# Routed experts of an SSM and mixture-of-experts kernel: gate and up weights become the stationary operand

## The chip, the cores and the metric

The kernel runs on one core of a Trainium2 chip. The metric is the device time of one launch in microseconds: the median of 3 runs. Lower is better. The profile is one further execution, taken by the hardware profiler; a profile has a span, which is the time from the core's first to its last instruction.

## What is computed

The input x has 128 sequences of 32 channels (heads) of 512 positions, all 32-bit floats. First, a state-space layer makes a kernel of 512 taps for each channel from its parameters, convolves each row causally with it, adds D times the input and sets everything from the sequence's length on to zero. The lengths lie between 78 and 453. Then the 4096 rows (sequence and channel) of 512 values are the tokens of a mixture of experts: 16 routed experts, 4 of them for each token, and a shared one for all.

```python
scores = sigmoid(x @ gate_w.T) + bias
topk_w, topk_idx = top_k(scores, 4)
topk_w = topk_w / (sum(topk_w) + 1e-20)
z   = silu(x @ Wg[e].T) * (x @ Wu[e].T)        # for every expert e of the token; 512 -> 256
out = sum over e of (z * weight of e) @ Wd[e].T   # 256 -> 512
out = out + silu(x @ Sg.T) * (x @ Su.T) @ Sd.T    # the shared expert
result = input + out
```

## The kernel before

The work has three stages. In the first (to about 122 us) TensorE convolves (L611), turns the results, and VectorE (DVE) works out the routing. The convolved rows go to a tensor in DRAM, `y_rows`, with the token's 16 expert weights behind each row's 512 values. They also stay on the chip, turned, as `yT`. The sequences are ranked by length, longest first.

In the second stage (to about 264 us, `unit_step`, L1114) the shared expert runs over `yT` in eight units of 512 tokens. Beside it the list of routed work is made (`slots`): tokens sorted by expert, in tiles of 128, each tile filled from one expert only. There are 128 to 143 tiles, depending on the routing.

The third stage (`turn_of`, L1267) runs over the tiles in a software pipeline that is written out by hand. Instructions are issued in the order of the program text on every engine (`tc.manual_schedule(engines=None)`, L1258), so what stands ahead of an instruction on its engine is read from the text. One step does this:

- POOL gathers the token rows of the tile four steps ahead from `y_rows` (L1037), with an indirect DMA.
- `tokens(step)`: TensorE transposes the 128 rows in blocks of 128 positions (L1168), ScalarE (ACT) copies the result to `yt` (L1174), and DVE picks each token's weight for the tile's expert, `wt` (L1175).
- `order(step - 2)`: SyncE (SP) marks when the rows that a tile adds to are free (L1251 to L1256).
- `turn(step - 2)`: two transposes of the tile's z (L1218), copied by DVE to `zT` (L1221).
- `inner(step - 1)`: the gate and up products. `yt` is the stationary operand, the weights move, 512 columns at once (gate and up side by side): one product for each position block (L1200). ACT takes the silu (L1211), DVE multiplies silu, up and token weight to z (L1212).
- `outer(step - 2)`: two down products (L1226), DVE's copy to `ob` (L1235), and POOL's indirect DMA that adds the rows to the output (L1236).
- `registers(step + 1)`: TensorE loads two numbers into registers: where the tile's expert lies in the ring of weights (`woff`, L1191), and how many blocks of 128 positions the longest sequence of the tile reaches, `k` from 1 to 4 (`ntk`, L1194).
- SP loads one more expert into the ring, if this tile is the first of its expert (L1286 to L1289).

The positions are stored in reverse, so that the used blocks are the last k of 4. `by_tiles` (L1044) makes the branches on k: two nested conditions with a full body for each value of k. A branch only exists for TensorE here; the other engines do the same work for every k. What a body signals to other engines has to be the same for each way through it, because those wait for a fixed count of TensorE's completions.

The weights of an expert (`WSZ`, 3072 columns on 128 partitions: gate and up in four blocks of 512, then down) lie in a ring of `R` = 8 places in the tile `store`. In the second stage `yT` and the shared expert's weights lie in the same tile. A place is loaded (L1145, L1146) once the units that it covers are through (`free_after`, L1107).

The 128 tiles that always exist are followed by those that the routing may need: there (`rest`, L1301) every engine first loads a register that says whether there is one more tile.

Of the kernel before, what the change touches and what calls it, by code (L numbers as in the profile page):

```python
# [28 lines left out]
F32 = mybir.dt.float32  # L29
# [3 lines left out]
AF = mybir.ActivationFunctionType  # L33
ALU = mybir.AluOpType
# [4 lines left out]
P = 128  # L39
B, H, L, N = 128, 32, 512, 64  # L40
E, TOPK, I = 16, 4, 256
KT = L // P
IT = I // P
# [4 lines left out]
NU = B // UB  # L48
TU = UB * H
NC2 = H * N // P  # L50
PAD = P
YW = L + E
R = 8
SPARE = 16
ONE_HOTS = 8
WARM = 16
# [7 lines left out]
WSZ = 2 * KT * I + IT * L  # L64
# [15 lines left out]
def ssm_moe_kernel(  # L80
# [15 lines left out]
    nc = tc.nc  # L96
# [3 lines left out]
    big = ctx.enter_context(tc.tile_pool(name="big", bufs=1))  # L100
    sp = ctx.enter_context(tc.tile_pool(name="sp", bufs=2))
    d1 = ctx.enter_context(tc.tile_pool(name="d1", bufs=1, space=bass.MemoryType.DRAM))
    ps_m = ctx.enter_context(tc.tile_pool(name="ps_m", bufs=2, space=PSUM))
    ps_g = ctx.enter_context(tc.tile_pool(name="ps_g", bufs=2, space=PSUM))
    ps_u = ctx.enter_context(tc.tile_pool(name="ps_u", bufs=2, space=PSUM))
# [16 lines left out]
    for j in range(2):  # L122
# [17 lines left out]

    store = big.tile([P, 3 * WSZ + KT * H * P], F32, tag="store", name="store")
    yT = store[:, 2 * WSZ : 2 * WSZ + KT * H * P].rearrange(
        "p (u k h b) -> p u k h b", u=NU, k=KT, h=H
    )
    w_sh = store[:, 2 * WSZ + KT * H * P :]
    ring_flat = store[:, : R * WSZ]
    y_rows = d1.tile([B * H, YW], F32, tag="y_rows", name="y_rows")
    out_bh = out[: B * H, :].rearrange("(b h) l -> b h l", h=H)  # L150
    y_bh = y_rows.rearrange("(b h) w -> b h w", h=H)
# [6 lines left out]
    def dep(of, on, why):  # L158
        tc.add_manual_dep(of.ins, on.ins.name, SYNC, reason=why)


    ident = const.tile([P, P], F32, tag="ident", name="ident")
# [584 lines left out]
    made = {}  # L747

    def slots():
# [53 lines left out]
        for n in range(1, KT):  # L803
# [12 lines left out]
        nc.vector.tensor_scalar(  # L816
            marks[:, 1, :], num[:E, :], float(R - 1), uend, ALU.add, ALU.is_ge
        )
        nc.vector.tensor_scalar(marks[:, 2, : R - 1], t_e[:, : R - 1], uend, None, ALU.is_ge)

# [13 lines left out]
        for k in range(TOPK):  # L834
# [10 lines left out]
        nc.tensor.matmul(  # L845
            pl[:, 1, : R - 1], lhsT=ones[:E, :], rhs=marks[:, 2, : R - 1], start=True, stop=True
        )
# [150 lines left out]
    with tc.manual_schedule(engines={mybir.EngineType.PE}):  # L998
        for h, n in [(0, 1), (1, 1), *((h, 2) for h in range(2, H, 2))]:
            tb, q = divmod(h, HB)  # L1000
# [18 lines left out]
    gp = ctx.enter_context(tc.tile_pool(name="gp", bufs=2))  # L1019
# [7 lines left out]
    def homes(pool, tag, shape, n):  # L1027

        return [pool.tile(shape, F32, tag=tag, name=f"{tag}_{i}", bufs=n) for i in range(n)]

    def at(tiles, t):
        return tiles[t % len(tiles)]
# [11 lines left out]
    def by_tiles(k_t, some):  # L1044


        with tc.If(k_t > 2) as many:
            with tc.If(k_t > 3) as all4:
                some(4)
            with all4.Else():  # L1050
                some(3)
        with many.Else():
            with tc.If(k_t > 1) as two:
                some(2)
            with two.Else():
                some(1)
# [49 lines left out]

    def free_after(j):  # L1107

        return min((max(j - 1, 0) * WSZ - 1) // (KT * TU), NU - 1)

    making = slots()
    gathered = 0
# [36 lines left out]
    w0s, k_ts = {}, {}  # L1149

    yt = homes(gp, "yt", [P, KT, P], 2)
    wts = homes(gp, "wt", [P, 1], 4)
    junks = homes(gp, "junk", [P, E], 2)
    sgs = homes(gp, "sgt", [P, I], 2)
    zs = homes(gp, "zt", [P, I], 2)
    zts = homes(gp, "zT", [P, IT, P], 2)
    p_t, p_gu = homes(ps_m, "m", [P, KT, P], 2), homes(ps_g, "g", [P, 2 * I], 2)
    p_z = homes(ps_u, "u", [P, IT, P], 2)

    marks = {}  # L1160

    def tokens(t):

        pt = at(p_t, t)

        def transposes(n):
            for q in range(KT - n, KT):
                nc.tensor.transpose(pt[:, q, :], at(yg, t)[:, q * P : (q + 1) * P], ident)  # L1168

        if t < len(p_t):  # L1170
            transposes(KT)
        else:
            by_tiles(k_ts[t], transposes)
        nc.scalar.copy(at(yt, t), pt)  # L1174
        nc.vector.scalar_tensor_tensor(  # L1175
            at(junks, t),
            epos,
            made["texp"][:, t : t + 1],
            at(yg, t)[:, L:],
            ALU.is_equal,  # L1180
            ALU.mult,
            accum_out=at(wts, t),
        )

    def in_ring(t, mm):
        for other in loads[t + 1 :]:
            tc.declare_no_dep(mm.ins, other.ins, reason="another place of the ring")
        dep(mm, loads[t], "the tile's expert")

    def registers(t):  # L1190
# [2 lines left out]
        )  # L1193
        k_ts[t] = nc.tensor.value_load(made["ntk"][0:1, t : t + 1], min_val=1, max_val=KT)  # L1194

    def inner(t):
        pgu = at(p_gu, t)
        def products(n):
            for q in range(KT - n, KT):
                mm = nc.tensor.matmul(  # L1200
                    pgu,
                    lhsT=at(yt, t)[:, q, :],
                    rhs=ring_flat[:, bass.ds(w0s[t] + q * 2 * I, 2 * I)],
                    start=(q == KT - n),
                    stop=(q == KT - 1),
                )
                in_ring(t, mm)

        by_tiles(k_ts[t], products)
        sg = at(sgs, t)  # L1210
        nc.scalar.activation(sg, pgu[:, :I], AF.Silu)  # L1211
        nc.vector.scalar_tensor_tensor(  # L1212
            at(zs, t), pgu[:, I:], at(wts, t), sg, ALU.mult, ALU.mult
        )

    def turn(t):
        for it in range(IT):
            nc.tensor.transpose(  # L1218
                at(p_z, t)[:, it, :], at(zs, t)[:, it * P : (it + 1) * P], ident
            )  # L1220
        nc.vector.tensor_copy(at(zts, t), at(p_z, t))  # L1221

    def outer(t):
        po = at(p_o, t)
        for it in range(IT):
            mm = nc.tensor.matmul(  # L1226
                po,
                lhsT=at(zts, t)[:, it, :],
                rhs=ring_flat[:, bass.ds(w0s[t] + WD + it * L, L)],
                start=(it == 0),  # L1230
                stop=(it == IT - 1),
            )
            in_ring(t, mm)
        ob = at(obs, t)
        nc.vector.tensor_copy(ob, po)  # L1235
        add = nc.gpsimd.indirect_dma_start(  # L1236
            out=out,
            out_offset=bass.IndirectOffsetOnAxis(ap=made["put"][:, t : t + 1], axis=0),
            in_=ob,
            in_offset=None,  # L1240
            compute_op=ALU.add,
        )
        dep(add, marks[t], "the rows it adds to")
        for other in adds:
            tc.declare_no_dep(add.ins, other.ins, reason="other rows, or behind the mark")
        adds.append(add)
# [11 lines left out]
    with tc.manual_schedule(engines=None):  # L1258

        dep(nc.tensor.nop(), parts_last[0], "in TensorE's order")  # L1260
        for u in range(NU):
            unit_step(u)
        for _ in making:
            pass
        registers(0)

        def turn_of(step):  # L1267
            if step + AHEAD < NT:
                gather(step + AHEAD)
            else:  # L1270
                nc.gpsimd.nop()
            if step < NT:
                tokens(step)
            if step >= 2:
                order(step - 2)
                turn(step - 2)
            if 1 <= step <= NT:
                inner(step - 1)
            if step >= 2:
                outer(step - 2)  # L1280
            if step + 1 < NT:
                registers(step + 1)
            if 1 <= step < NT:

                t = step - 1
                e = nc.sync.value_load(made["lexp"][0:1, t : t + 1], min_val=0, max_val=E - 1)  # L1286
                to = nc.sync.value_load(made["loff"][0:1, t : t + 1], min_val=0, max_val=(R - 1) * WSZ)
                go = nc.sync.value_load(made["load"][0:1, t : t + 1], min_val=0, max_val=1)
                ld = load_expert(e, ring_flat[:, bass.ds(to, WSZ)], go)  # L1289
                for other in loads:  # L1290
                    tc.declare_no_dep(ld.ins, other.ins, reason="another place of the ring")
                loads.append(ld)

        turn_of(0)
        unit_step(NU)
        for step in range(1, NT_MIN + 2):
            if step == LAST_DRAIN:
                nc.gpsimd.drain(fusable=False)
            turn_of(step)

        def rest(step):  # L1301

            if step == NT + 2:
                return
            _, (some,) = nc.values_load_multi_w_load_instructions(
                made["full"][0:1, step - 2 : step - 1], min_val=0, max_val=1
            )
            with tc.If(some > 0):
                turn_of(step)
                rest(step + 1)  # L1310

        rest(NT_MIN + 2)
# [51 lines left out]
```

## Time and profile before

| | |
|---|---|
| median of 3 runs | 913.76 us (913.17 to 913.97) |
| the profiled execution | 913.5 us |
| its span, mean granted TensorE clock | 911.8 us, 0.992 |
| busy share of the span: TensorE products, its weight loads, DVE, ACT, POOL | 96%, 49%, 45%, 21%, 46% |
| the routed stage | from 264 us to about 900 us |
| products L1200 and L1226, transposes L1168 and L1218: records | 742, 536, 373, 268 |

PE is TensorE and PEld its weight loads; PEldq and PEq are its sequencer, which reads the instructions. A group's line reads: source line, engine, operation, output and inputs by their names, number of records; then busy microseconds and the mean nanoseconds of one; then the idle time before them and what ended it. The ends of products are modelled, so their mean is longer than their pace. The chain of work that ended last goes back from the last instruction to what released it; a line of it reads: start, microseconds, engine, output, line, number. A 32-bit product shows as two records, each with its weight load, a transpose as one; a few records can be missing.

### The profile page before, as it was taken

To read this page: it belongs to the slowest core of one execution; us is meant where nothing else is said; L and a number is where in the kernel's file an instruction comes from. 1 tells how busy PE (TensorE), PEld (TensorE's weight loads), DVE (VectorE), ACT (ScalarE), POOL (GpSimd) and SP (SyncE) were. 2 spreads that over 40 slices of the span, in tenths; PEclk is the share of its full clock that TensorE was granted. 3 is DMA by queue.
4 is the path that set the end of the run, shared out by engine and by line. 5 is a ranking of instruction groups with operands and counts; after the bars stand their busy time and mean duration, and the time that the engine had idled before them with its cause. 6 is when DMAs were issued, how large, how long until landed. Compare 5 with 4: busy or idle time off the path is not lost.

```text
span 911.8 us, 14680 instructions
## 1 busy us (share of the span) xinstructions
PE 872.7 (96%) x2976; PEld 445.0 (49%) x2976; DVE 414.7 (45%) x1488; ACT 188.8 (21%) x379; POOL 420.1 (46%) x372
## 2 busy tenths in 40 slices
PE   2999999999999999999999999999999999999994
PEld 1677654444444444445444444444444545444441
DVE  8988664968802334333342334333333323344332
ACT  1222221111231112211221122112221112122221
POOL 2210011422473556645564456545654455566554
PEclk9999999999999999999999999999999999999997
DMA  5688576786698667766677667656756556667575
GB/s 198 216 279 274 185 242 193 207 197 124 125 218 202 141 114 131 165 135 114 120 140 171 113 110 140 114 110 108 141 108 108 107 96 117 109 129 136 105 127 98
DMA packets 54710, 136.03 MB, mean 149 GB/s; under 512 B 12432, under 2 KB 12592, under 8 KB 50992
## 3 DMA queue, kind: packets, MB, share of 16 engines
q0 software_dynamic: 36256, 89.77, 53.4%
q1 hardware_dynamic: 14096, 36.15, 11.8%
q10 hardware_dynamic: 4224, 8.39, 2.5%
q8 instruction: 76, 1.25, 0.5%
q14 instruction: 58, 0.48, 0.2%
HBM read 288.08 MB, written 60.64 MB: 382 GB/s over the span
## 4 chain that ended last, share of the span: by engine, by line
PE 92%; DVE 2%; SPq 2%; issue 2%; POOL 0%; ACT 0%; DMA 0%; ACTq 0%; DVEq 0%; POOLq 0%
PE g L1200 35%; PE o L1226 24%; PE o L1087 6%; PE py L611 6%; PE g L1072 5%; PE u L1072 4%; PE m L1168 4%; PE u L1218 3%; PE pt L635 1%; PE pa L902 1%; PE parts L656 1%; PE pg L673 1%; SPq L1251 1%; DVE wq L269 0%; PE py L446 0%
## 5 line engine op out<-in xcount | busy, mean ns | idle before, releaser
L1200 PE MATMUL g<-store,yt 128*128 x742 | 343.1, 596 | 1.9 <-issue 1.4
L1236 POOL DMA_INDIRECT out<-ob,put x134 | 212.1, 1583 | 234.5 <-DVE junk L1175 186.8
L1226 PE MATMUL o<-store,zT 128*128 x536 | 252.0, 592 | 0.0
L1212 DVE SCALAR_TENSOR_TENSOR zt<-g,wt,sgt 128x256 f32<-128x256 f32 x135 | 65.3, 484 | 305.2 <-ACT sgt L1211 301.6
L1200 PEld LDWEIGHTS g<-store,yt 128*128 128x128 f32 x742 | 130.3, 190 | 118.9 <-issue 117.8
L1226 PEld LDWEIGHTS o<-store,zT 128*128 128x128 f32 x536 | 101.4, 190 | 128.7 <-issue 124.3
L1037 POOL DMA_INDIRECT yg<-y_rows,get x140 | 138.1, 986 | 49.8 <-issue 30.8
L1235 DVE COPY ob<-o 128x512 f32<-128x512 f32 x134 | 92.6, 691 | 109.3 <-PE o L1226 99.5
L1174 ACT COPY yt<-m 128x512 f32<-128x512 f32 x136 | 79.6, 585 | 226.0 <-PE m L1168 216.2
L1211 ACT ACTIVATE sgt<-g 128x256 f32<-128x256 f32 x135 | 51.7, 383 | 268.8 <-PE g L1200 227.5
L1096 POOL DMA_INDIRECT out<-ob,unit_rows x32 | 50.2, 1567 | 92.6 <-ACT ob L1094 57.6
L1168 PEld LDWEIGHTS m<-ident,yg 128*128 128x128 f32 x373 | 48.7, 141 | 72.2 <-issue 71.7
L611 PE MATMUL py<-strip,xt 128*128 128x192 f32 (+7 forms) x256 | 63.6, 403 | 0.0
L1168 PE MATMUL m<-ident,yg 128*128 128x128 f32 x373 | 63.0, 273 | 0.5 <-issue 0.4
L1087 PE MATMUL o<-store,z 128*128 128x512 f32 x128 | 57.6, 597 | 0.6 <-issue 0.6
L1221 DVE COPY zT<-u 128x256 f32<-128x256 f32 x134 | 56.2, 419 | 0.5 <-issue 0.4
L611 PEld LDWEIGHTS py<-strip,xt 128*128 128x128 f32 x256 | 44.2, 194 | 18.5 <-issue 13.2
L1218 PE MATMUL u<-ident,zt 128*128 128x128 f32 x268 | 51.2, 273 | 0.6 <-DVE zt L1212 0.6
L1072 PE MATMUL g<-store 128*128 128x512 f32 x92 | 42.9, 601 | 1.5 <-issue 1.2
L1072 PE MATMUL u<-store 128*128 128x512 f32 x92 | 42.2, 593 | 0.0
L914 DVE TENSOR_SCALAR cols<-tpos_h,stl,tok 128x143 f16<-128x143 f16 x128 | 41.4, 328 | 0.0
L1087 PEld LDWEIGHTS o<-store,z 128*128 128x128 f32 x128 | 23.4, 190 | 26.3 <-issue 26.2
(285 smaller groups left out, 490.6 us busy)
## 6 DMA issues: line engine op xcount, KB each, us to landing
store<-in_w_all SPq DMA_DIRECT2D x143, 1536.0 KB
xt<-in_x_t SPq DMA_DIRECT2D x8, 1024.0 KB
y_rows<-yb ACTq DMA_DIRECT2D x8, 1024.0 KB
out<-in_x POOLq DMA_DIRECT2D x8, 1024.0 KB
strip<-kd SPq DMA_DIRECT2D x7, 1024.0 KB
yg<-y_rows,get POOLq DMA_INDIRECT x140
out<-ob,put POOLq DMA_INDIRECT x134
strip<-kd SPq DMA_DIRECT2D x4, 256.0 KB
```

The costliest lines, as they stand in the source:

```text
L611: nc.tensor.matmul(py[:, c0 : L - jt * P], lhsT=xt[:, jt, q, :], rhs=strip[tb][:, q, jt * P + c0 :], start=(jt == 0), stop=(jt == KT - 1 o ...
L1037: nc.gpsimd.indirect_dma_start(out=at(yg, t), out_offset=None, in_=y_rows[:, :], in_offset=bass.IndirectOffsetOnAxis(ap=made["get"][:, t : ...
L1072: nc.tensor.matmul(ps[it], lhsT=w_sh[:, c0 : c0 + P], rhs=yT[:, u, kt, :, :].rearrange("p h b -> p (h b)"), start=(kt == KT - n), stop=(kt ...
L1087: nc.tensor.matmul(po, lhsT=at(zu, u)[:, it, q * P : (q + 1) * P], rhs=w_sh[:, c0 : c0 + L], start=(it == 0), stop=(it == IT - 1),)
L1168: nc.tensor.transpose(pt[:, q, :], at(yg, t)[:, q * P : (q + 1) * P], ident)
L1174: nc.scalar.copy(at(yt, t), pt)
L1200: mm = nc.tensor.matmul(pgu, lhsT=at(yt, t)[:, q, :], rhs=ring_flat[:, bass.ds(w0s[t] + q * 2 * I, 2 * I)], start=(q == KT - n), stop=(q = ...
L1212: nc.vector.scalar_tensor_tensor(at(zs, t), pgu[:, I:], at(wts, t), sg, ALU.mult, ALU.mult)
L1218: nc.tensor.transpose(at(p_z, t)[:, it, :], at(zs, t)[:, it * P : (it + 1) * P], ident)
L1226: mm = nc.tensor.matmul(po, lhsT=at(zts, t)[:, it, :], rhs=ring_flat[:, bass.ds(w0s[t] + WD + it * L, L)], start=(it == 0), stop=(it == IT ...
L1235: nc.vector.tensor_copy(ob, po)
L1236: add = nc.gpsimd.indirect_dma_start(out=out, out_offset=bass.IndirectOffsetOnAxis(ap=made["put"][:, t : t + 1], axis=0), in_=ob, in_offse ...
```

## The change

The gate and up products swap their operands. The weights become the stationary operand, four squares of 128 by 128 for each position block, and the tokens move, 128 columns at a time. The result is z with its 256 features on the partitions, which is the form that the down products need: `turn` and its transposes go away.

[...] `fetch(step)`, at the start of a step, copies the expert's gate and up weights from the ring to one of two tiles `fixed`: ACT copies the blocks 0 and 1, DVE the blocks 2 and 3, each 1024 columns, after a register load of `woff` on its own engine. The copy for a tile is issued one step before its products.

With features on the partitions the token's weight can't be applied at z any more; DVE's product for z becomes a plain product of silu and up, and the weight is applied at the output's copy, where tokens lie on the partitions.

The branches on k are written anew: the last block always; if k > 1, block 1 if k > 2, block 0 if k > 3, and block 2 at the end; otherwise the last block alone. The two tiles take room, so the ring has 7 places instead of 8, and `yT` begins at column 2048 of the tile instead of 6144 (`Y0`), which changes when a place may first be loaded.

```diff
-R = 8
+R = 7
...
-    store = big.tile([P, 3 * WSZ + KT * H * P], F32, tag="store", name="store")
-    yT = store[:, 2 * WSZ : 2 * WSZ + KT * H * P].rearrange(
-        "p (u k h b) -> p u k h b", u=NU, k=KT, h=H
-    )
-    w_sh = store[:, 2 * WSZ + KT * H * P :]
-    ring_flat = store[:, : R * WSZ]
+    store = big.tile([P, R * WSZ], F32, tag="store", name="store")
+    Y0 = R * WSZ - WSZ - KT * H * P
+    yT = store[:, Y0 : Y0 + KT * H * P].rearrange("p (u k h b) -> p u k h b", u=NU, k=KT, h=H)
+    w_sh = store[:, Y0 + KT * H * P :]
+    ring_flat = store
+
+    fixed = [big.tile([P, KT, 2 * I], F32, tag=f"fixed{i}", name=f"fixed{i}") for i in range(2)]
...
-        return min((max(j - 1, 0) * WSZ - 1) // (KT * TU), NU - 1)
+        return min(((j + 1) * WSZ - Y0 - 1) // (KT * TU), NU - 1)
...
+    def fetch(t):
+
+        for engine, copy, q0 in (
+            (nc.scalar, nc.scalar.copy, 0),
+            (nc.vector, nc.vector.tensor_copy, KT // 2),
+        ):
+            w0 = engine.value_load(made["woff"][0:1, t : t + 1], min_val=0, max_val=(R - 1) * WSZ)
+            half = KT // 2 * 2 * I
+            op = copy(
+                at(fixed, t)[:, q0 : q0 + KT // 2, :].rearrange("p k w -> p (k w)"),
+                ring_flat[:, bass.ds(w0 + q0 * 2 * I, half)],
+            )
+            in_ring(t, op)
+
     def inner(t):
-        pgu = at(p_gu, t)
-        def products(n):
-            for q in range(KT - n, KT):
-                mm = nc.tensor.matmul(
-                    pgu,
-                    lhsT=at(yt, t)[:, q, :],
-                    rhs=ring_flat[:, bass.ds(w0s[t] + q * 2 * I, 2 * I)],
-                    start=(q == KT - n),
-                    stop=(q == KT - 1),
-                )
-                in_ring(t, mm)
-
-        by_tiles(k_ts[t], products)
+
+        pgu, w = at(p_gu, t), at(fixed, t)
+
+        def products(q, start, stop):
+
+
+            for g in range(2):
+                for it in range(IT):
+                    c0 = g * I + it * P
+                    first, end = (g, it) == (0, 0), (g, it) == (1, IT - 1)
+                    nc.tensor.matmul(
+                        pgu[:, g, it, :],
+                        lhsT=w[:, q, c0 : c0 + P],
+                        rhs=at(yt, t)[:, q, :],
+                        start=start and first,
+                        stop=stop and end,
+                    )
+
+        last, more = KT - 1, k_ts[t]
+        with tc.If(more > 1) as several:
+            products(last, True, False)
+            with tc.If(more > 2):
+                products(1, False, False)
+                with tc.If(more > 3):
+                    products(0, False, False)
+            products(2, False, True)
+        with several.Else():
+            products(last, True, True)
         sg = at(sgs, t)
-        nc.scalar.activation(sg, pgu[:, :I], AF.Silu)
-        nc.vector.scalar_tensor_tensor(
-            at(zs, t), pgu[:, I:], at(wts, t), sg, ALU.mult, ALU.mult
-        )
-
-    def turn(t):
-        for it in range(IT):
-            nc.tensor.transpose(
-                at(p_z, t)[:, it, :], at(zs, t)[:, it * P : (it + 1) * P], ident
-            )
-        nc.vector.tensor_copy(at(zts, t), at(p_z, t))
+        nc.scalar.activation(sg, pgu[:, 0], AF.Silu)
+        nc.vector.tensor_mul(at(zs, t), sg, pgu[:, 1])
...
-                lhsT=at(zts, t)[:, it, :],
+                lhsT=at(zs, t)[:, it, :],
...
-        nc.vector.tensor_copy(ob, po)
+        nc.vector.tensor_scalar(ob, po, at(wts, t), None, ALU.mult)
...
             if step < NT:
+                fetch(step)
                 tokens(step)
             if step >= 2:
                 order(step - 2)
-                turn(step - 2)
             if 1 <= step <= NT:
                 inner(step - 1)
```

## The prediction

> **What bounds the kernel now.** I read the chain that ended last, then the groups, then the order of time inside the routed stage, which runs from 264 us to about 900 us of the 911.8 us span. The chain, by engine and by line:
>
> ```profile
> PE 92%; DVE 2%; SPq 2%; issue 2%; POOL 0%; ACT 0%; DMA 0%; ACTq 0%; DVEq 0%; POOLq 0%
> PE g L1200 35%; PE o L1226 24%; PE o L1087 6%; PE py L611 6%; PE g L1072 5%; PE u L1072 4%; PE m L1168 4%; PE u L1218 3%; PE pt L635 1%; PE pa L902 1%; PE parts L656 1%; PE pg L673 1%; SPq L1251 1%; DVE wq L269 0%; PE py L446 0%
> ```
>
> TensorE is the bound, and the changed products (L1200) with the removed transposes (L1218) are 38% of the chain. The groups show what one instruction costs on each engine:
>
> ```profile
> L1200 PE MATMUL g<-store,yt 128*128 x742 | 343.1, 596 | 1.9 <-issue 1.4
> ...
> L1235 DVE COPY ob<-o 128x512 f32<-128x512 f32 x134 | 92.6, 691 | 109.3 <-PE o L1226 99.5
> L1174 ACT COPY yt<-m 128x512 f32<-128x512 f32 x136 | 79.6, 585 | 226.0 <-PE m L1168 216.2
> ...
> L1221 DVE COPY zT<-u 128x256 f32<-128x256 f32 x134 | 56.2, 419 | 0.5 <-issue 0.4
> L1218 PE MATMUL u<-ident,zt 128*128 128x128 f32 x268 | 51.2, 273 | 0.6 <-DVE zt L1212 0.6
> ```
>
> The 596 ns is a latency. The chain between 600 and 610 us shows the pace, in a step whose tile needs k=3 position blocks:
>
> ```profile
> 599.89 2.58 PE g L1200 x6
> 602.47 1.72 PE o L1226 x4
> 604.19 0.33 PE m L1168 x3
> 604.51 0.22 PE u L1218 x2
> 604.73 2.58 PE g L1200 x6
> ```
>
> Six records in 2.58 us are 0.43 us each: a 32-bit product is two records, each with its own weight load. A transpose is one record of 0.11. So a step costs 0.11k + 0.22 + 0.86k + 1.72 us: 4.84 for k=3, 5.81 for k=4, 3.88 for k=2. The chain has 28 steps with k=4, 54 with k=3 (mean 4.854), 44 with k=2 (mean 3.947) and 9 with k=1 (about 3.25). Only short steps have holes, as here around 453 us (k=2):
>
> ```profile
> 452.43 0.22 PE m L1168 x2
> 452.65 0.22 PE u L1218 x2
> 452.87 0.10 issue
> 452.97 1.95 PE g L1200 x4
> ```
>
> "Issue" is the instruction front end of TensorE (its sequencer), which works in order. Its own records:
>
> ```profile
> L1191 PEldq TENSOR_LOAD <-woff x137: 297/306/662, 261.8 to 897.1; - x137
> ...
> L1194 PEldq SEQ_ASSERT  x137: 18/18/18, 263.2 to 898.4; - x137
> ...
> L1048 PEldq COMPARE_BRANCH  x364: 65/179/358, 122.7 to 879.2; - x182
> ```
>
> The two register loads of a step take it from 261.8 to 263.2; over all steps the records give 1.38 us. A branch not taken is 65 ns, one taken 170 to 210, and about 60 ns pass before the next instruction: 0.12 and 0.235 us. A product costs about 0.08 us to issue. The sequencer needs 3 to 3.5 us for a short step, so it hides only while it runs ahead of the array.
>
> **The change, part by part.** Removed: 268 transposes (L1218) at 0.109 us, -29.2 us of TensorE, and their copy (L1221) on DVE, which no longer holds the sequencer.
>
> Changed: for each block, one product with 512 moving columns (2 x 0.429 = 0.858 us) becomes four with 128 (8 records). The nearest row is an ordinary 32-bit product of 128x128 by 128 columns, here with its loads:
>
> ```profile
> 79.05 0.30 PEld L736 LDWEIGHTS cw_ps<-cw,to_row 128*128 128x128 f32 x2
> 79.16 0.39 PE L736 MATMUL cw_ps<-cw,to_row 128*128 128x128 f32 x2
> ```
>
> Two loads of 0.19 in 0.30 us start 0.11 apart: the load of one record lies under the product before it. Record to record I read 0.112. So 0.896 per block, and over the 371 blocks of the chain +14 us. The Trainium skill (TensorE: Matmul & The Clock Gate, Back-to-back issue gap) gives about 81 ns for such a pair at 128 columns; that would make the blocks 78 us cheaper than today (8 x 0.081 x 371 = 240 against 318). The row decides: 0.112. By pace alone the change is worth -29 + 14 = -15 us.
>
> **Added, and deciding: a wait of TensorE for itself.** Before, each k had its own full branch. Now the blocks stand in nested conditions: last; if k>1, if k>2 block 1, if k>3 block 0; then block 2. TensorE's completion count must be equal on all ways, so in the instructions as built the empty side of "k>2" and "k>3" holds an event wait of TensorE on its own count, until every earlier product is complete, and then adds the missing 8 or 4. With k=3 or 2 (98 steps) the sequencer stands there, with block 2 and all later work behind it, and the queue to the array runs dry. k=4 and k=1 have no such wait.
>
> No row of before shows this wait blocking, so it is built from neighbours. How fast an engine wakes behind a product:
>
> ```profile
> 599.73 2.74 PE L1200 MATMUL g<-store,yt 128*128 x6
> ...
> 602.51 0.38 ACT L1211 ACTIVATE sgt<-g 128x256 f32<-128x256 f32 x1 [2.16 <-PE g L1200]
> ```
>
> 602.47 to 602.51: 0.04 us. A 128-column record lasts 0.273, so the wait ends 0.31 after the last record's start; the wait record and the step to the next instruction are 0.076, a load 0.106. For k=2 the next record starts 0.49 after the last instead of 0.112: a hole of 0.38. For k=3 a taken jump (0.235) lies between: 0.62. Lower end 0.2 (the count arrives without latency), upper end 0.9 (a late jump; the longest took 0.36).
>
> Then the lost lead. From the end of the wait, k=3: jump 0.235, four products 0.32, jump 0.235, address, wait and the two down products 0.38, register loads 1.38, two branches 0.36. The first transpose issues 3.0 after the wait and starts at 3.11; the array ran out at 0.43 + 0.90 + 1.72 = 3.05. Transposes end at 3.44. Meanwhile jump 0.235, branch 0.12, wait 0.08: the next block's load issues at 3.57, product at 3.67. Two blocks are 16 records, the last starting at 5.35; the next wait ends at 5.66. Period 5.66 against 4.854: +0.81. The same for k=2: product at 3.45, eight records, 4.54 against 3.947: +0.59. k=4: 0.44 + 32 x 0.112 + 1.72 = 5.74, -0.07. k=1 stays bound by the sequencer, 0.
>
> Sum: 54 x 0.81 + 44 x 0.59 - 28 x 0.07 = 43.7 + 26.0 - 2.0 = +68 us. Span 911.8 + 68 = 980. The profiled run took 913.5 (1.7 more than its span), as good as the median 913.76, so 982. A second rule speaks to the branches: the skill (Advanced Engine Details and Errata, Control Flow Timing) has 51 ns for an unconditional and 108 ns for a comparing branch. With these, an estimate for k=3 loses some 0.3 us of the 0.81 and the total about 25 us. The rows have 65 not taken and 170 to 210 taken; I stay with the rows.
>
> **The other parts.** Copies of weights: ACT from 268 ns (L740, 128 columns) to 585 (512) is 0.83 ns per column, so 1024 columns take about 1.0 us. DVE by 419 and 691 is 1.24 at most. Each also loads a register (L1305: ACT 0.28, DVE 0.30 to 0.76) and needs about 0.4 around it. ACT then has 0.7 + 1.0 + 0.58 + 0.38 = 2.7 us per step. DVE has 1.2 + 1.24 + 0.31 (token weight) + 0.48 (silu product) + 0.69 (output with the weight: same shape and source as L1235) = 3.9. Both lie under steps of 4.5 and more, and a copy has until the next but one up product, over a step later: cost 0. In the 9 steps with k=1 DVE could lack 0.7: up to 6 us. Queued behind a late copy would be yt, silu, the output and its add on POOL.
>
> Ring of 7: places lie lower under yT, so of the loads now issued together at 170 to 174 us two go then and the others up to the last unit; the first use is at 264 and six experts stay ahead: 0. POOL's adds and gathers, and SP's order marks, are the same instructions: 0.
>
> **Rivals.**
> 1. *The wait costs nothing* (the sequencer arrives late enough, or counts are kept otherwise). Then k=3 is 4.73, k=2 about 3.85 by the sequencer, k=4 5.74: -13 us, 901. Against it: a sequencer ahead of the array, which the gapless k=3 steps show, always finds the product before it unfinished. It decides for faster only if holes and lost lead together stay under 0.13 us per step.
> 2. *The copies become the bound*: if DVE's copy took twice its value, its step is 5.1 us; k=2 steps go to 5.1 and k=1 too: +25 + 17, 1024. Against: DVE was busy 18 of 50 us in the stage.
> 3. *Weight loads don't overlap* (0.19 each): 2968 x 0.078 = +231, over 1200. L736 and the transposes, 0.109 apart, speak against it.
> 4. *A small drain*: lower end of the hole and a sequencer that catches up: +0.1 to +0.3 per step, 925 to 943.
>
> **How the numbers follow.** Forecast 0.80, rival 4 0.06, rivals 2 and 3 0.07, rival 1 0.07. The ends: each of 98 steps 0.35 cheaper gives 947, 0.35 dearer 1016; I take 942 to 1020. Faster 0.06, within 0.2% (what a measurement here can tell) 0.01, slower 0.93.
>
> **What would show it.** In the chain, k=3 steps near 5.7 and k=2 near 4.5 us while k=4 falls to 5.74; up records 0.112 apart; a hole of 0.4 to 0.6 us before block 2 in every step with k=2 or 3, with an event wait of TensorE's sequencer at the condition's line; "issue" holes before the transposes and the first up product. Wrong if TensorE stays gapless at k=3, if it waits for the fixed weights' ACT or DVE copy, or if k=4 steps grow too.

## The result and the profile after

The changed kernel takes 989.38 us (median of 4 runs, 988.29 to 992.88). The kernel before, run alongside, takes 913.87 us. The ratio is 1.0829, with a 95% interval of 1.0809 to 1.0849: 8% slower. The profiled execution took 989.9 us, with a span of 988.2 us and a granted clock of 0.996 (0.992 before), so the clock is not what slows it.

The groups of instructions name the same engine as before, and the new copies beside it:

```profile
L1220 PE MATMUL g<-yt,fixed 128*128 128x128 f32 x2968 | 385.3, 280 | 33.0 <-PEq L1233 21.9
L1220 PEld LDWEIGHTS g<-yt,fixed 128*128 128x128 f32 x2968 | 349.1, 191 | 66.1 <-issue 56.6
L1255 POOL DMA_INDIRECT out<-ob,put x134 | 246.5, 1840 | 276.4 <-DVE ob L1254 228.5
L1245 PE MATMUL o<-store,zt 128*128 x536 | 252.2, 593 | 0.0
...
L1203 ACT COPY fixed<-store 128x1024 f32 x136 | 142.1, 1045 | 68.5 <-ACT sgt L1239 56.3
...
L1254 DVE TENSOR_SCALAR ob<-o,wt 128x512 f32<-128x512 f32 x134 | 100.6, 751 | 117.9 <-PE o L1245 90.6
...
L1203 DVE COPY fixed<-store 128x1024 f32 x136 | 95.5, 702 | 23.8 <-DVE ob L1254 12.9
```

The up products (L1220) number 2968 records, which is 371 blocks of 8. Idle time stands before them, put down to line 1233 of TensorE's sequencer. Line 1233 is the condition "k > 3". POOL's add (L1255) has grown to 1840 ns, though its instruction is the same as before, where its row was:

```profile
L1236 POOL DMA_INDIRECT out<-ob,put x134 | 212.1, 1583 | 234.5 <-DVE junk L1175 186.8
```

The list of waits has TensorE's idle time by what ended it (microseconds in total, times, longest):

```profile
PE g L1220 <- PEq L1233: 21.9, 51, 0.5
...
PE m L1167 <- issue: 10.3, 30, 1.0
```

The first line holds 51 of the 54 steps with k = 3. The modelled ends of products hide part of each hole, so 21.9 us is less than what the holes cost. The second line is the holes ahead of the token transposes.

One step with k = 3 in order of time:

```profile
642.73 0.49 PE L1167 MATMUL m<-ident,yg 128*128 128x128 f32 x3
643.06 1.95 PE L1220 MATMUL g<-yt,fixed 128*128 128x128 f32 x16
645.44 1.16 PE L1220 MATMUL g<-yt,fixed 128*128 128x128 f32 x8 [0.42 <-PE g L1220]
```

Sixteen records at 0.112 us from 643.06 would let the next one start at 644.85. It starts at 645.44, and the second record of that block follows another 0.1 us late. The sequencer's own records at the two conditions (nanoseconds lowest/median/highest) show what stands there:

```profile
L1233 PEldq COMPARE_BRANCH  x164: 65/179/361, 271.2 to 956.1; - x164
L1233 PEldq EVENT_SEMAPHORE  x54: 51/51/51, 278.0 to 955.9; - x54
...
L1231 PEldq EVENT_SEMAPHORE  x44: 51/51/51, 353.6 to 966.4; - x44
```

An event wait occurs 54 times at "k > 3" and 44 times at "k > 2": once for each step with k = 3 and each with k = 2. The record of the wait is short (51 ns) because it begins only when the wait is over: 0.32 us (median) after the start of the last product before it, which itself lasts 0.275.

From first transpose to first transpose, sorted by k (mean us; k = 4 as the median, since one of its steps has the start of the stage in it):

| k | steps | before | after | forecast | difference, all steps |
|---|---|---|---|---|---|
| 3 | 54 | 4.854 | 5.972 | 5.66 | +60.4 us |
| 2 | 44 | 3.947 | 4.469 | 4.54 | +22.9 |
| 1 | 8 | 3.49 | 3.20 | no change | -2.3 |
| 4 | 28 | 5.81 | 5.73 | 5.74 | -0.7 (with +1.5 of the stage's first two steps) |

Together +80. The stage begins 2 us earlier (261.9 against 263.8) and ends 2 us closer to the last instruction (13.9 against 15.9), so the span grows by 76.4 us.

The chain that ended last, which carried the reading of before, is of no use here. It breaks off at the place that costs the time:

```profile
issue 1%; POOL 0%; PE 0%; SPq 0%; POOLq 0%
```

TensorE waits there for a count that TensorE itself raises, and the chain names nothing earlier than 961 us, the last steps of the stage. The steps were therefore taken from the order of time.

### The profile page after: what moved, and what is told of

The parts are those of the page before. It is cut to its first block, busy times and chain, and to the rows that moved or that the text cites. A ratio compares the mean times of both kernels' runs of the same rounds, so it can differ in the third digit from the quotient of the medians.

```text
span 988.2 us, 20102 instructions
## 1 busy us (share of the span) xinstructions
PE 906.5 (92%) x4934; PEld 609.8 (62%) x4934; DVE 464.1 (47%) x1490; ACT 329.9 (33%) x515; POOL 456.2 (46%) x372
## 5 line engine op out<-in xcount | busy, mean ns | idle before, releaser
L1220 PE MATMUL g<-yt,fixed 128*128 128x128 f32 x2968 | 385.3, 280 | 33.0 <-PEq L1233 21.9
L1220 PEld LDWEIGHTS g<-yt,fixed 128*128 128x128 f32 x2968 | 349.1, 191 | 66.1 <-issue 56.6
L1255 POOL DMA_INDIRECT out<-ob,put x134 | 246.5, 1840 | 276.4 <-DVE ob L1254 228.5
L1245 PE MATMUL o<-store,zt 128*128 x536 | 252.2, 593 | 0.0
L1240 DVE TENSOR_TENSOR zt<-sgt,g 128x256 f32<-128x256 f32 x135 | 56.9, 421 | 307.3 <-ACT sgt L1239 293.3
L1203 ACT COPY fixed<-store 128x1024 f32 x136 | 142.1, 1045 | 68.5 <-ACT sgt L1239 56.3
L1254 DVE TENSOR_SCALAR ob<-o,wt 128x512 f32<-128x512 f32 x134 | 100.6, 751 | 117.9 <-PE o L1245 90.6
L1245 PEld LDWEIGHTS o<-store,zt 128*128 128x128 f32 x536 | 91.6, 191 | 64.1 <-issue 64.1
L1167 PEld LDWEIGHTS m<-ident,yg 128*128 128x128 f32 x373 | 43.6, 140 | 105.1 <-issue 103.5
L1203 DVE COPY fixed<-store 128x1024 f32 x136 | 95.5, 702 | 23.8 <-DVE ob L1254 12.9
```

The source lines that it names most:

```text
L1203: op = copy(at(fixed, t)[:, q0 : q0 + KT // 2, :].rearrange("p k w -> p (k w)"), ring_flat[:, bass.ds(w0 + q0 * 2 * I, half)],)
L1220: nc.tensor.matmul(pgu[:, g, it, :], lhsT=w[:, q, c0 : c0 + P], rhs=at(yt, t)[:, q, :], start=start and first, stop=stop and end,)
L1240: nc.vector.tensor_mul(at(zs, t), sg, pgu[:, 1])
L1245: mm = nc.tensor.matmul(po, lhsT=at(zs, t)[:, it, :], rhs=ring_flat[:, bass.ds(w0s[t] + WD + it * L, L)], start=(it == 0), stop=(it == IT ...
L1254: nc.vector.tensor_scalar(ob, po, at(wts, t), None, ALU.mult)
L1255: add = nc.gpsimd.indirect_dma_start(out=out, out_offset=bass.IndirectOffsetOnAxis(ap=made["put"][:, t : t + 1], axis=0), in_=ob, in_offse ...
```

## The experiments

Ratios are against the kernel before on the same chip. The theory: TensorE's wait for its own completions, in the empty sides of the nested conditions, is the loss, and the rest of the change is a small gain. The rival: the operand swap itself (copies, queue pressure, POOL's longer adds) costs something too.

**Own branches.** The changed kernel, with a full branch for each k as before.

```diff
-        last, more = KT - 1, k_ts[t]
-        with tc.If(more > 1) as several:
-            products(last, True, False)
-            with tc.If(more > 2):
-                products(1, False, False)
-                with tc.If(more > 3):
-                    products(0, False, False)
-            products(2, False, True)
-        with several.Else():
-            products(last, True, True)
+        def blocks(n):
+            for q in range(KT - n, KT):
+                products(q, q == KT - n, q == KT - 1)
+
+        by_tiles(k_ts[t], blocks)
```

> The changed kernel, but each k has its own full branch again, so TensorE has no wait for itself; operands, copies and the rest as changed. Theory (the wait and the lost lead are the whole loss): k=3 steps 4.73 us, k=2 about 3.85, k=4 5.74, so 895 to 903 us, faster than before. Rival (copies of the weights, 128-column products or register loads hold TensorE by themselves): k=3 stays above 5.3 us and the time above 950.

Measured: 904.05 us (903.32 to 904.62), ratio 0.9899 (0.9878 to 0.992), 1 us above the expected range. k = 3 takes 4.72 us, k = 2 3.89, k = 4 5.73. The chain is whole again:

```profile
601.35 1.72 PE o L1240 x4
603.06 0.33 PE m L1167 x3
603.39 2.68 PE g L1220 x24
606.07 1.72 PE o L1240 x4
607.79 0.33 PE m L1167 x3
```

TensorE goes from one kind of work to the next without a hole, and 24 up records take 2.68 us, 0.112 each. So the swap, its copies and the smaller ring together are a gain of 9 us (the forecast's pace alone had 15), and the nested conditions cost 85 of the changed kernel's 989. This version is 1% faster than the kernel before.

**The nested conditions alone**, in the kernel before: weights still move, z is still transposed.

```diff
...
-        by_tiles(k_ts[t], products)
+        last, more = KT - 1, k_ts[t]
+        with tc.If(more > 1) as several:
+            product(last, True, False)
+            with tc.If(more > 2):
+                product(1, False, False)
+                with tc.If(more > 3):
+                    product(0, False, False)
+            product(2, False, True)
+        with several.Else():
+            product(last, True, True)
```

> The kernel before, with moving weights, transposes of z and no copies, but with the nested conditions of the changed kernel (last block; k>1: k>2: block 1; k>3: block 0; block 2). Theory (the wait alone makes the loss): k=3 steps 4.85 to about 5.75 us, k=2 3.95 to about 4.65, so about 990 us, between 965 and 1005. Rival (the loss comes with the swapped operands or the copies): under 925.

Measured: 1009.31 us (1007.55 to 1010.94), ratio 1.1043 (1.1013 to 1.1073): a little above the expected range. Two steps with k = 2 in order of time:

```profile
603.49 1.08 PE L1199 MATMUL g<-store,yt 128*128 x2
604.87 1.12 PE L1199 MATMUL g<-store,yt 128*128 x2 [0.30 <-PEq L1211]
605.83 1.88 PE L1234 MATMUL o<-store,zT 128*128 x4
```

Two records at 0.43 would end at 604.35 and the next starts at 604.87. Over all steps the hole is 0.56 us for k = 2 and 0.79 for k = 3, larger than in the changed kernel (0.39 and 0.69, below). The drain is not the reason: in both kernels the wait ends 0.21 us later than the next record would have started at the pace. But here the address of the moving weights is worked out in a register behind the wait: for k = 2 the next weight load starts 0.25 us after the wait's record, in the changed kernel 0.08. The step grows by more than its hole: k = 3 by 1.05 us, k = 2 by 0.95. The loss comes with the conditions, whatever the products are. What lies above the expected range goes with a second effect, which the changed kernel's trace shows too: register loads that take far longer than usual ("held" below), of which this kernel has the most (91 of 277). They are the subject of the next run.

**What the sequencer's register loads wait for.** TensorE's two register loads take 0.30 us each in the kernel before, and 4 of its 277 are over 0.40. In the changed kernel 67 of 277 are over 0.40, by 35 us in all. In the step shown above the load of k, a record of TensorE's sequencer, stands beside POOL's instructions in order of time:

```profile
L1193 PEldq TENSOR_LOAD <-ntk x1: 831/831/831, 646.8 to 646.8; - x1
```

```profile
643.97 1.98 POOL L1255 DMA_INDIRECT out<-ob,put  x1 [1.62 <-DVE ob L1254]
646.25 0.99 POOL L1038 DMA_INDIRECT yg<-y_rows,get  x1 [0.30 <-issue]
```

The load begins at 646.83, while POOL works on the gather of 646.25, and ends at 647.66, 0.42 us behind the gather's end at 647.24. So the theory of the next run was that a load which begins during a gather is held. But 135 of the 140 gathers of this kernel start 0.30 us behind an add, as this one does, so the load also begins 0.88 us behind the add's end at 645.95, and ends 1.71 us behind it. To test the theory, the gather was moved ahead of the add in POOL's order, behind the scaling of the output:

```diff
-        nc.vector.tensor_scalar(ob, po, at(wts, t), None, ALU.mult)
+        scaled = nc.vector.tensor_scalar(ob, po, at(wts, t), None, ALU.mult)
+        ahead = t + 3 + AHEAD
+        if ahead < NT:
+            dep(gather(ahead), scaled, "in POOL's order")
         add = nc.gpsimd.indirect_dma_start(
...
-            if step + AHEAD < NT:
+            if step < 3:
                 gather(step + AHEAD)
```

> The changed kernel, with POOL's gather issued before the add of the same step instead of behind it (it waits for the output's copy), so that it lies where TensorE's sequencer stands at its wait and loads no register. Theory (a register load that begins while POOL issues a gather is held to about 0.4 us behind its end, which is what makes k=3 steps 5.97 us instead of 5.66): long register loads of TensorE fall from 67 to under 15, k=3 steps to about 5.7, time 989 to about 974. Rival (the register loads are slow because of the copies of weights on ACT and DVE): the count stays near 67 and the time within 4 us of 989.

Measured: 965.84 us (963.56 to 967.68), ratio 1.0565 (1.0534 to 1.0596), which is 23.5 us below the changed kernel and lower than expected. Long loads fall from 67 to 23 (not below 15, as expected), k = 3 from 5.97 to 5.54 us. TensorE in order of time:

```profile
626.72 1.16 PE L1220 MATMUL g<-yt,fixed 128*128 128x128 f32 x8 [0.43 <-PEq L1233]
627.72 1.88 PE L1245 MATMUL o<-store,zt 128*128 x4
629.44 0.49 PE L1167 MATMUL m<-ident,yg 128*128 128x128 f32 x3
629.77 1.97 PE L1220 MATMUL g<-yt,fixed 128*128 128x128 f32 x16
632.15 0.60 PE L1220 MATMUL g<-yt,fixed 128*128 128x128 f32 x3 [0.42 <-PEq L1233]
```

The hole before the last block is still there (L1233), while the second hole, ahead of the transposes and the first up product, is gone. Up to about a third of the loss (23.5 of 76 us) thus came from held register loads.

That the gather is what holds them is not borne out, though. This trace has gathers that no add precedes closely, and two loads in a row:

```profile
596.41 1.58 POOL L1258 DMA_INDIRECT out<-ob,put  x1 [0.30 <-SPq L1310]
599.22 1.38 POOL L1038 DMA_INDIRECT yg<-y_rows,get  x1 [1.23 <-DVE ob L1254]
```

```profile
L1190 PEldq TENSOR_LOAD <-woff x1: 975/975/975, 598.7 to 598.7; - x1
...
L1193 PEldq TENSOR_LOAD <-ntk x1: 298/298/298, 600.1 to 600.1; - x1
```

The first load begins 0.7 us behind the add's end at 597.99 and half a microsecond ahead of the gather, and is held. The second begins and ends inside the gather and is not. Loads over 0.40 us, of all loads that begin at the place named:

| kernel | 0.35 to 1.25 us behind an add's end | of these, no gather at the load's start | elsewhere, during a gather | all others |
|---|---|---|---|---|
| before | 4 of 4 | 1 of 1 | none | 0 of 273 |
| changed | 65 of 67 | 1 of 2 | 0 of 5 | 2 of 205 |
| nested conditions alone | 87 of 89 | none | 3 of 6 | 1 of 182 |
| gather moved | 23 of 23 | 12 of 12 | 0 of 41 | 0 of 213 |
| own branches, gather moved (below) | 57 of 60 | 24 of 27 | 4 of 111 | 3 of 106 |

So what counts is the time since POOL's add ended. In the kernel before, a load simply rarely fell there; the hole moves it there. Moving the gather ahead also moved the add: in steps with k = 3 it ended 2.90 us behind the step's first transpose and now ends at 4.48 (medians), behind the loads at 3.41 and 4.12. The conditions cause both parts of the loss: the wait makes the hole, and the late sequencer meets the time behind the add. This edit moves both of POOL's instructions and shortens the add (to 1597 ns) together; the next run takes the add's length alone.

**The copy on one engine.** ACT copies all 2048 columns, DVE none.

```diff
-        for engine, copy, q0 in (
-            (nc.scalar, nc.scalar.copy, 0),
-            (nc.vector, nc.vector.tensor_copy, KT // 2),
-        ):
...
+        w0 = nc.scalar.value_load(made["woff"][0:1, t : t + 1], min_val=0, max_val=(R - 1) * WSZ)
+        op = nc.scalar.copy(
+            at(fixed, t).rearrange("p k w -> p (k w)"),
+            ring_flat[:, bass.ds(w0, KT * 2 * I)],
+        )
+        in_ring(t, op)
```

> The changed kernel, with all four blocks of weights copied by ACT (one copy of 2048 columns, about 1.9 us); DVE copies none. Theory (DVE's copy of weights makes POOL's add 1.84 us instead of 1.58, which moves the gather behind it into the register loads): the add is back at 1.58 us, the gather comes 0.26 us earlier, fewer than 30 long register loads, time 974 to 982. Rival (the longer add has another cause): the add stays near 1.84 us and the time within 4 us of 989 or above, since ACT has 3.6 us per step.

Measured: 978.18 us (975.43 to 983.94), ratio 1.0698 (1.0669 to 1.0728). From the groups of this kernel:

```profile
L1198 ACT COPY fixed<-store 128x2048 f32 x136 | 258.3, 1899 | 60.5 <-ACT sgt L1234 56.0 <-issue 2.8 <-DVE zt L1235 0.9
L1250 POOL DMA_INDIRECT out<-ob,put x134 | 212.2, 1583 | 301.0 <-DVE junk L1174 259.3 <-issue 37.4 <-DVE ob L1249 4.0
```

The add is back at 1583 ns, so the expected cause of its growth holds: DVE's copy. The other half of the expectation missed. Long loads did not fall but rose to 80, and k = 3 steps are 0.17 us shorter although they are held as often (51 of 54 steps). The time came out where it was expected, by another way. The add ends earlier (2.62 against 2.90 us behind the first transpose) and the held loads are a little shorter (per held step 0.46 us beyond the usual 0.30 of each, against 0.54); whether that is all of the 11 us stays open.

**Own branches with the moved gather**, both edits above in one kernel.

> The kernel with its own full branch for each k and POOL's gather ahead of the add: both causes away. Theory (20 long register loads are left in the version with own branches, and they make its k=2 steps 3.89 us in the mean against a median of 3.72): long loads under 8, k=2 mean about 3.75, time 897 to 901 us. Rival (the rest of k=2 is the sequencer's own work, not the held loads): 902 to 905 us.

Measured: 909.04 us (902.71 to 910.87, 9 runs), ratio 0.9938 (0.9915 to 0.996). The expectation failed, and the time is above its rival's range too: no gain over own branches alone (0.9899). There, only 20 loads were long; here there are 64, and 40 of 44 steps with k = 2 have one. Without the wait the sequencer comes to its loads early in the step, for k = 2 at 1.10 us behind the first transpose, while the add, pushed back by the moved gather, ends at 4.49 us, which is 0.5 us into the next step. So the same move takes long loads away in one kernel and makes them in another. That agrees with the time behind the add, and not with the gather: of 111 loads that begin during a gather but not behind an add, 4 are long. The held loads cost little here (k = 2 3.97 us against 3.89), presumably because TensorE still has work queued while a load is held; that was not tested.

**Half of the waits.** Full branches for k = 1 and 2; above 2 the condition is nested, so that only k = 3 has an empty side.

```diff
-        with tc.If(more > 1) as several:
-            products(last, True, False)
-            with tc.If(more > 2):
-                products(1, False, False)
-                with tc.If(more > 3):
-                    products(0, False, False)
-            products(2, False, True)
-        with several.Else():
-            products(last, True, True)
+        with tc.If(more > 2) as many:
+            products(last, True, False)
+            products(1, False, False)
+            with tc.If(more > 3):
+                products(0, False, False)
+            products(2, False, True)
+        with many.Else():
+            with tc.If(more > 1) as two:
+                products(last, True, False)
+                products(2, False, True)
+            with two.Else():
+                products(last, True, True)
```

> The changed kernel with a full branch for k=1 and k=2, and the nested condition only above 2: of the 98 steps with a wait, the 54 with k=3 keep it. Theory (each waiting step pays for itself): k=3 steps 5.9 to 6.0 us as with all waits, k=2 near 3.9 as with none, so 904 + 54 x 1.25 = about 971 us. Rival (a few waits are enough to lose TensorE's lead for all steps, or the waits hide each other): k=2 stays near 4.4 and the time above 982, or k=3 falls below 5.5 and the time below 955.

Measured: 951.58 us (949.51 to 954.53), ratio 1.0407 (1.0391 to 1.0423). The only wait left, in the sequencer's records, is that of k = 3:

```profile
L1232 PEldq EVENT_SEMAPHORE  x54: 51/51/51, 280.6 to 921.2; - x54
```

k = 2 takes 3.85 us, as with own branches; k = 3 takes 5.76. The loss goes with the waits, step by step. The time is below the expected 971 us and also below the 955 that the rival named, but k = 3 did not fall below the rival's 5.5 us. It is less than expected because the hole is 0.39 us here and not 0.69: no jump follows the empty side in this form, and I had carried the jump over from the changed kernel. That measures the jump: 0.30 us of the changed kernel's 0.69. A hole of 0.39 still makes the step 1.04 us longer than own branches (4.72), and 48 of the 54 steps again have a held load: these take 5.82 us in the mean, the six others 5.28.

## Why the prediction was right, point by point

The forecast was 982 us in a range of 942 to 1020, slower at 0.93. The cause it named is the one that the runs show: taking the wait away (own branches) gives 904, adding it to the kernel before gives 1009. The sum was +68 us of span and is +76. So the mechanism was right; that a single step with k = 3 came out as near as it did is in part luck, as two errors of its working go against each other (below).

- *Pace.* 0.112 us per 128-column record, from one pair of rows: measured 0.112, with the weight load (191 ns) hidden. The 0.081 that the prediction took from the Trainium skill (TensorE: Matmul & The Clock Gate, Back-to-back issue gap) does not hold for these products; with it, the blocks alone would have been 78 us cheaper than before, and own branches gained 9 us in all. k = 4, which has neither wait nor jump, shows the pace alone: 5.73 us against a forecast of 5.74.
- *The wait and its place.* Event waits at the two conditions, 54 and 44 times, none for k = 1 and 4: right. The hole for k = 2 (how much later the block's last record starts than the pace would have it) is 0.39 us, forecast 0.38. At the block's first record it shows as 0.32, at its second the rest is added.
- *The hole for k = 3, forecast 0.62, is 0.69.* The term that was too small is the wait record and the step behind it: 0.149 us from the record's start to the jump, where the forecast had 0.076. The price of the jump held: 0.23 us from its record to the next weight load, forecast 0.235.
- *The lost lead was too large.* Its listed terms do not add up to what was carried: up to the first transpose they give 2.91 us (2.99 with the wait's record), and from there to the next block's load 0.435, where the text goes from 3.0 to 3.57. And "a product costs about 0.08 us to issue" was too dear: four issue within 0.08 us together (behind the wait of k = 2 the first weight load starts at 0.08 us and the jump behind all four products at 0.15). In the changed kernel only three k = 3 steps have no held load, too few to read. With the early gather there are 50, and they take 5.46 us (median): the pace of 4.73, the hole of 0.69, and 0.04 of lost lead where the forecast had 0.29.
- *The register loads were too cheap.* The forecast carried 1.38 us for both through every step, from records that nearly all lie away from the time behind an add (273 of 277). In the changed kernel 51 of 54 steps with k = 3 have a held load, and they average 5.99 us, about 0.5 more than the 5.46. This is the largest term missing from the sum (with the hole and the lost lead, the step's whole growth over own branches); the sentence "POOL's adds and gathers ... are the same instructions: 0" is where it should have stood. It counted POOL's own time and not what stands behind POOL's add for a load on another engine's sequencer.
- *The errors go against each other* for k = 3: 5.66 forecast, +0.07 hole, -0.25 lead, +0.5 held loads, 5.97 measured. For k = 2, where only 8 of 44 steps are held, the lead's error stays and the forecast of 4.54 is above the 4.47.
- *The copies.* Hidden, as forecast: 1.045 us on ACT (forecast 1.0), 0.70 on DVE (at most 1.24). DVE's rows used for the bound read PSUM, at 1.35 ns per column (691 ns for 512); this copy, between two places in SBUF, takes 0.69 ns per column (702 ns for 1024). Whether the weights could be read as the stationary operand straight from the ring, without copies, no run here shows. Steps with k = 1 became shorter rather than longer (3.20 us against 3.49 in the mean; the prediction's 3.25 was their median before).
- *The rivals.* "The wait costs nothing" had 901 for a kernel without the loss, and own branches came to 904; its mistake is only in what the wait does. Copies as the bound and unhidden weight loads are excluded by 904 as well. "A small drain" needed 0.1 to 0.3 us per step; it was 0.5 and 1.1.

## What to carry to other kernels

A conditional without an else is not free on an engine whose completions others count: its empty side made TensorE wait until all its products were through. That cost more than the hole of 0.4 to 0.7 us: in the changed kernel a step with k = 3 is 1.25 us longer than with own branches, of which 0.7 is the hole and about 0.5 goes with held register loads, which the late sequencer ran into. A full body for each case kept TensorE gapless at k = 3 and turned 8% slower into 1% faster. Where a sequencer has lost its lead, every instruction that it issues lies on the path: then look at what its register loads run beside and behind.

## What the runs showed of the hardware

*Register loads behind an indirect add.* A register load of TensorE's sequencer that began 0.35 to 1.25 us behind the end of POOL's indirect add was held in 391 of 418 cases over all eight kernels, typically until 1.70 us behind the add's end, instead of taking 0.30. Elsewhere during a gather it was held in 10 of 173, and at all other times in 17 of 1625. What of the add holds it was not tried; the mechanism is open.

*DVE's copy and POOL's add.* An add that began while DVE's 1024-column copy ran ended 1.45 us (median of 98) behind the copy's end. In the step shown above DVE has, in order of time:

```profile
643.79 0.69 DVE L1203 COPY fixed<-store 128x1024 f32 x1
```

The copy ends at 644.48 and the add that began at 643.97 at 645.95. The adds that met no copy, and most of those that began ahead of one, took 1.58 us, and without DVE's copy all did (the run with ACT's copies). With the gather moved it is the gather that meets the copy: the 82 that began while it ran took 1.38 us (median), 0.99 elsewhere. The Trainium skill (Advanced Engine Details and Errata, VectorE Performance Modes) says that VectorE's second SBUF port is shared with GPSIMD, and that vector instructions which use both ports and GPSIMD instructions block each other. The runs agree as to this copy; that the port is the cause is argued from the page and not shown here.
